# A decoder layer on one core: how far ahead the scores run, when weights are squared, and where small tiles lie

## The chip, the cores and the metric

The kernel runs on one core of a Trainium2 chip. A core has TensorE (PE) for matmuls, whose results land in PSUM, a memory of eight banks; VectorE (DVE), ScalarE (ACT) and GpSimd (POOL) for elementwise work; and DMA queues, here issued by SyncE (SP). The engines run side by side, each takes its own instructions strictly in order, and semaphores make one wait for another. The metric is the device time of one execution in microseconds, lower is better.

## The reference

One pre-norm decoder layer on x of 8 batches x 128 tokens x 512 features in fp32:

```python
x = x + _L0_attn_ref(_layernorm(x), w_q, w_k, w_v, w_o)
x = x + _L0_xattn_ref(ctx, ctx, _layernorm(x))
x = x + _L0_ffn_ref(_layernorm(x), gate_*, up_*, down_*)
```

The first line is causal self-attention with 32 query heads of 128 features in 8 groups; the four query heads of a group share one key and value head. The second is a small attention of x over ctx for each batch. The third is a gated FFN, 512 to 1376 and back, whose three weight matrices come as packed 4-bit words: of each int32, nibble k is shifted out and masked, a zero point plus one is taken off, and the rest is multiplied by a scale for each group of 128 rows.

## The kernel before

**Precision and the cost of it.** Matmuls are in fp16, with each operand split into a high and a low half; `mm3` (L160 to L166) does one product as three matmuls, high x high (L164), high x low (L165) and low x high (L166). `split` (L117) makes the halves: a cast on ACT (L118), a subtraction on DVE or POOL (L121). Weights come in fp32. Before they are split they are scaled by a power of two, which comes from their sum of squares: `sumsq` (L244) squares a block on ACT and adds it up along the row (L262), `scales_parts` (L276) casts the sums on DVE (`sb`, L285), adds them over the partitions with a one-column matmul into a PSUM tile `ps_n` (L289, L292) and makes the scale on DVE (L298, L306, L314). `soft_scale` (L327) makes from the scales of q and k the factor that goes into the softmax: two small multiplications (L331) and a reciprocal (L339) on DVE. `convert` (L350) then multiplies the weights on POOL (L355) and splits them, cast on ACT, subtraction on POOL: `wqh`/`wql`, `wkh`/`wkl`, `woh`/`wol`. The raw q weights of a group (`rawq`, 1 MB) and the raw output weights (`rawo`) have one buffer each, so the next group's fetch waits until the last conversion has read it.

**Steps.** The attention is 64 steps, one for each head group and batch (`steps`, L1051). A step has three parts on PE:
- `att_s` (L587): the scores, 12 small matmuls into `ps_sc`; masking and row maximum on DVE (L608), exponentials on ACT (L565), sums' reciprocal on DVE (L573), the multiplications on POOL (L575, L622), a split into `pb`, and a DMA that transposes `pb` to `pt` (L636).
- `att_v` (L639): `pt` times the values, five matmuls into `ps_at` (the first at L645), evicted to `ah` (ACT) and `al` (DVE).
- `att_o` (L653): `ah`, `al` times the output weights, 12 matmuls of 512 columns into `ps_o`, and the residual update `xr` on DVE (L662).
Beside these a step carries a piece of the projections of a later group (`proj_piece`, L1111: 12 matmuls of 512 columns for one query head, at times those of k or of v too).

**How far ahead.** `step` (L1367) issues `att_s` and `proj_piece` of step i + 1 up to step SOON = 14, of i + 2 from there to BACK = 42, and of i + 1 again afterwards; at step BACK itself none is issued. From step TAIL = 53 on `tail_step` (L1335) takes over, again with a distance of one, and adds the cross-attention and the start of the FFN. The loop at L1387 issues behind each step what was booked for it: with `at` (L1117) the fetches, squares, scales and conversions of later groups (L1120 to L1147), with `at_x` (L1062) the loads, squares and scales of ctx (`c_load`, `sumsq("c")`, `c_prep`, L1065 to L1068), and from step 8 to step 42 one `dequant` chunk each, 35 in all.

**Dequantization.** `dequant` (L785) loads a chunk of packed words (`qr`) and its zero points (`zi`) by DMA; DVE shifts and masks (L807) into the SBUF tile `qi` (one buffer) and subtracts (L811) into the fp16 weights `nfg`, `nfu`, `nfd`.

**PSUM.** `bank` (L189) hands out banks by tag: two each for "j" (projections), "s" (scores), "a" (`ps_at`, `ps_n` and later the transposes of the output) and "o" (`ps_o`).

**Who sets the order.** The Tile framework schedules: the code's order is a priority, and each engine's instructions are put where the framework expects them to be ready. `in_order` pins an order by hand, for all engines at the start and for PE and POOL from step 52 on; `issue_after` (L124) puts one instruction behind another of its engine, so the squares behind the exponentials of their step and the conversions behind the softmax's multiplications (`pace`). What the scheduler made of it is read from the built program.

Of the kernel before, what the change touches and what calls it, by code (L numbers as in the profile page):

```python
# [12 lines left out]
I32 = mybir.dt.int32  # L13
# [4 lines left out]
P = 128  # L18
HQ = 64
B = 8  # L20
H = 512
KT = 4
NG = 8
GH = 4
# [29 lines left out]
def tile_decoder(  # L54
# [129 lines left out]


    psum = pool("psum", space=PSUM)
    BANKS = {"j": 2, "s": 2, "a": 2, "o": 2}

    def bank(tag, shape, name):  # L189
        return psum.tile(shape, F32, name=name, tag=tag, bufs=BANKS[tag])  # L190


# [83 lines left out]
    def scales_parts(kind, g, cols=None):  # L276

        ss = raw_t["ss", kind, g]  # L280
        n = ss.shape[1]
        c0, c1 = cols or (0, n)
        m = c1 - c0
        sb = small.tile([P, m], BF16, name="sb", tag=f"sb{m}")
        nc.vector.tensor_copy(sb, ss[:, c0:c1])  # L285
        ps = bank("a", [P, GH], "ps_n")
        w = m if kind == "q" else 1
        if w == m:
            nc.tensor.matmul(ps[:, :w], ones, sb, start=True, stop=True)  # L289
        else:  # L290
            for i in range(m):
                nc.tensor.matmul(  # L292
                    ps[:, :1], ones, sb[:, i : i + 1], start=i == 0, stop=i == m - 1
                )
        yield
        norm = ONORM if kind == "o" else WNORM
        r = small.tile([P, w], F32, name="r", tag=f"r{w}")
        nc.vector.tensor_scalar(  # L298
            r.bitcast(I32),
            ps[:, :w].bitcast(I32),  # L300
            0x7F000000,
            1,
            ALU.bitwise_and,
            ALU.logical_shift_right,
        )
        nc.vector.tensor_scalar(r, r, ROOT, 2.0**64 / norm, ALU.max, ALU.mult)  # L306
        if kind == "c":
            sc_t[kind, g] = scx[:, g : g + 1]
        if (kind, g) not in sc_t:
            sc_t[kind, g] = small.tile(  # L310
                [P, GH if kind == "q" else 1], F32, name="sc" + kind, tag="sc" + kind
            )
        sc = sc_t[kind, g]
        nc.vector.reciprocal(sc[:, c0:c1] if kind == "q" else sc, r)  # L314
        yield
# [11 lines left out]
    def soft_scale(g):  # L327
        two = small.tile([P, GH // 2], F32, name="soft", tag="soft")
        for i in range(2):
            rows = slice(i * HQ, (i + 1) * HQ)  # L330
            nc.vector.tensor_scalar(  # L331
                two[rows],
                sc_t["q", g][rows].rearrange("p (a i) -> p a i", i=2)[:, :, i],
                sc_t["k", g][rows],
                -(ASCALE**2) / SCALE,
                ALU.mult,
                ALU.mult,
            )
        nc.vector.reciprocal(two, two)  # L339
        soft_t[g] = two  # L340
# [444 lines left out]
    def dequant(m, g, c0, c1, after, pts=None):  # L785
        qsrc = quant[m][0]
        n = c1 - c0
        rows = min(16, qsrc.shape[0] - g * 16)
        p = rows * 8
        qr = deqp.tile([P, H], I32, name="qr", tag="qr", bufs=2)  # L790
        load_q = nc.sync.dma_start(
            qr[:p, :n],
            qsrc[g * 16 : g * 16 + rows, c0:c1]
            .rearrange("r n -> r () n")
            .to_broadcast([rows, 8, n]),
        )
        zi = deqp.tile([P, H], I32, name="zi", tag="zi", bufs=2)
        row = zrow[m] + g
        load_z = nc.sync.dma_start(
            zi[:p, :n],  # L800
            zt["d"][row : row + 1, c0:c1].to_broadcast([p, n]),
        )
        if pts:
            issue_after(load_q, pts)
            issue_after(load_z, pts)
        qi = deqp.tile([P, H], I32, name="qi", tag="qi", bufs=1)
        ins = nc.vector.tensor_scalar(  # L807
            qi[:p, :n], qr[:p, :n], sh[:p], 15, ALU.logical_shift_right, ALU.bitwise_and
        )
        issue_after(ins, after)  # L810
        nc.vector.scalar_tensor_tensor(  # L811
            nf[m][:p, g, c0:c1], qi[:p, :n], -1.0, zi[:p, :n], ALU.add, ALU.subtract
        )
# [250 lines left out]

    for b in range(B):  # L1065
        at_x(XC + b, lambda b=b: c_load(b))
        at_x(XC + b + 1, lambda b=b: sumsq("c", b, 0, 0))
        at_x(XC + b + 3, lambda b=b: c_prep(b))  # L1068
        done = steps.index((NG - 1, b))
        tail_x.setdefault((done + 1, 0), []).append(lambda b=b: xA(b))  # L1070


        if b >= HB:
            if b % 2:
                two = b - 1, b
                tail_x.setdefault((done + 2, 1), []).append(
                    lambda two=two: [xB(b) for b in two]
                )
                tail_x.setdefault((done + 3, 2), []).append(
                    lambda two=two: [(xC(b), h3_load(b)) for b in two]  # L1080
                )
            continue
        tail_x.setdefault((done + 2, 1), []).append(lambda b=b: xB(b))
        tail_x.setdefault((done + 3, 2 if b < HB - 1 else 0), []).append(
            lambda b=b: (xC(b), h3_load(b))
        )
# [33 lines left out]
    for g in range(1, NG):  # L1120
        u0 = units.index((g, 0))
        c = HB * (u0 - 2) - (g > 2)
        if g > 1:
            m = c - HB
            at(m, lambda g=g: fetch_wk(g))
            at(m + 1, lambda g=g: (fetch_wq(g), sumsq("k", g, 0, 0)))
            at(m + 2, lambda g=g: (sumsq("q", g, 0, 0), sumsq("q", g, 0, 1)))
            at(m + 3, lambda g=g: (sumsq("q", g, 0, 2), sumsq("q", g, 0, 3)))
            at(m + 3, lambda g=g: (scales("q", g), scales("k", g), soft_scale(g)))
        for j in range(GH):  # L1130
            at(c + j, lambda g=g, j=j: prep_wq(g, j))
        at(c + 1, lambda g=g: prep_wk(g))
        c = HB * (u0 - 1)
        m = c - HB
        at(m, lambda g=g: fetch_wo(g))
        at(m + 1, lambda g=g: sumsq("o", g, 0, 0, 2))
        at(m + 2, lambda g=g: sumsq("o", g, 1, 0, 2))
        at(m + 3, lambda g=g: (scales("o", g), out_scale(g)))
        for j in range(GH):
            at(c + j, lambda g=g, j=j: prep_wo(g, j))  # L1140
        if g % 2 == 0:
            c = HB * (u0 - 3) - (g > 2)
            at(c - 2, lambda g=g: fetch_wv(g // 2))
            at(c - 1, lambda g=g: sumsq("v", g // 2, 0, 0))
            at(c, lambda g=g: scales("v", g // 2))
            at(c + 2, lambda g=g: prep_wv(g // 2, 0))
            at(c + 3, lambda g=g: prep_wv(g // 2, 1))  # L1147
# [214 lines left out]
        for f in tail_x.pop((i, 1), ()):  # L1362
            f()

    SOON, BACK = 14, 42

    def step(i):  # L1367
        g, b = steps[i]
# [17 lines left out]
    soft_scale(1)  # L1386
    for i in range(len(steps)):  # L1387
        known = len(nc.cur_bb.bb.instructions)
        if i == XC:
            deqp.release()  # L1390
            xc = pool("xc", 2, side="right", reuse_waits="tile")
        if i == FFN_MEM:
            rawp.release()
            fp = pool("fp", 2, reuse_waits="tile")
            xa = pool("xa", 2, reuse_waits="tile")
        if i == FFN0:
            xt.update(s="a", o="a")
        pace["dma"] = pt_dma[steps[i + 1]] if i >= TAIL and steps[i + 1 :] and steps[i + 1] in pt_dma else None
        paced = (tail_step if i >= TAIL else step)(i)
        pace["exp"], pace["mul"] = paces[steps[i + (SOON < i < min(BACK, len(steps) - 1))]]  # L1400
        for f in todo.pop(i, ()):
            f()
        if 3 <= i < 6:
            col_scales("gud"[i - 3], paced)
        if i == 0:
            zeros_load()
        if i == 1:
            scales_load()
        if 1 <= i < 5:
            zeros((2 * (i - 1), 2 * (i - 1) + 1), paced)  # L1410
        if i == 5:
            zeros_store()
        if i in chunk_steps:
            dequant(*chunks[chunk_steps.index(i)], paced, pt_dma[steps[i + 1]] if i == chunk_steps[0] else None)
        if i == 6:
            inter_scale()
        for f in x_steps.pop(i, ()):
            f()
        if i < 5 * HB:
            traced_after(known, last_h.ins.engine, last_h)  # L1420
        if i == TAIL - 1:
            pins = [in_order((e,)) for e in (mybir.EngineType.PE, mybir.EngineType.Pool, )]
            for pin in pins:
                pin.__enter__()
        if i == FFN0 - 1 + 0:
            pins[0].__exit__(None, None, None)
# [60 lines left out]
```

## Time and profile before

| what | value |
|---|---|
| three runs | 656.52, 656.67, 656.84 us; median 656.67 |
| the profiled execution | 655.96 us, its span 654.2 us |
| granted PE clock | 0.998 of full speed |
| first PE matmul of step 0's, 20's, 42's and 53's `att_v` | 53.7, 203.9, 361.0, 452.0 us |
| DVE: unpacking, L807, 128x512 | 26 x 725 ns |
| DVE: subtraction, L811, 128x512 | 26 x 792 to 955 ns |
| DVE: soft factor, L331 | 16 x 412 ns |
| ACT: square of 128x512, L262 | 627 ns and 188 ns for reading the sum |
| DMA: rawq, 1 MB | 5.8 us from issue to landing |
| DMA: pt | 2.7 us from issue to landing |

The span runs from the first to the last instruction of the profiled execution. "Busy" is the time in which an engine has an instruction under way; for PE, whose matmuls overlap, a row's duration is longer than its distance to the next one, so the start times tell more than the durations. In a group's line, the idle time is that of its engine just before the group's instructions, with what ended it. A line of the code can be that of a helper, so tiles are named beside it.

### The profile page before, as it was taken

What the parts mean: (1) busy time and instruction counts of PE and PEld (TensorE: products, weight loads), DVE (VectorE), ACT (ScalarE), POOL (GpSimd) and SP (SyncE); (2) the same over time, 40 slices, a digit from 0 to 9 for tenths busy, and PEclk for the clock granted to TensorE, in tenths of its full rate; (3) what the DMA queues carried; (4) which work ended last, traced back from release to release, by engine and by line L of the source; (5) the groups of instructions that cost most, each with busy time, mean ns of one, the idle gap of its engine ahead of it and who ended that gap; (6) DMA issues with size and microseconds to landing.
All of it is one profiled execution on the core that took longest, in us unless ns stands there. A gap on an engine that the chain in (4) does not pass through costs nothing.

```text
span 654.2 us, 12431 instructions
## 1 busy us (share of the span) xinstructions
PE 629.8 (96%) x3992; PEld 342.3 (52%) x3992; DVE 465.6 (71%) x1475; ACT 439.3 (67%) x1238; POOL 380.8 (58%) x586
## 2 busy tenths in 40 slices
PE   8789999999999999999999999999999989999996
PEld 6455545565655555565555465556544434445443
DVE  6846676665767866576777555767776768988986
ACT  5687677465667675566667576866566478867674
POOL 7757477563747883475489395734577247612521
PEclk9999999999999999999999999999999999999999
DMA  9287254943763756355636414343544242102002
GB/s 316 48 171 170 75 72 122 229 105 79 190 164 88 187 137 160 95 168 127 151 94 167 143 41 122 66 92 74 89 67 68 39 93 50 31 19 65 1 1 64
DMA packets 117773, 69.34 MB, mean 106 GB/s; under 512 B 84190, under 2 KB 100593, under 8 KB 117708
## 3 DMA queue, kind: packets, MB, share of 16 engines
q1 hardware_dynamic: 117708, 68.55, 44.0%
q8 instruction: 31, 0.51, 0.3%
q14 instruction: 34, 0.28, 0.2%
HBM read 42.12 MB, written 2.20 MB: 68 GB/s over the span
## 4 chain that ended last, share of the span: by engine, by line
PE 73%; DVE 8%; DMA 6%; ACT 6%; POOL 4%; issue 2%; SPq 1%; DVEq 0%; ACTq 0%; POOLq 0%
PE ps_o L166 7%; PE ps_o L164 7%; PE ps_o L165 7%; PE ps_q L164 7%; PE ps_q L165 7%; PE ps_q L166 7%; PE ps_c L1181 6%; PE ps_c L1182 6%; DMA rawq<-in_L_attn_w_q_dram 3%; DMA pt<-pb 2%; PE ps_v L164 2%; PE ps_v L166 2%; PE ps_v L165 2%; PE ps_k L165 2%; PE ps_k L166 2%
## 5 line engine op out<-in xcount | busy, mean ns | idle before, releaser
L565 ACT ACTIVATE s<-s,negm 128x64 f32<-128x64 f32 (+1 forms) x256 | 93.1, 365 | 51.5 <-DVE negm L608 50.8
L164 PE MATMUL ps_q<-hT,wqh 128*128 128x512 f16 (+1 forms) x260 | 97.7, 376 | 1.6 <-DVE ql L121 1.6
L164 PE MATMUL ps_o<-woh,ah 128*128 128x512 f16 x256 | 97.0, 379 | 1.2 <-ACT ah L118 1.2
L166 PE MATMUL ps_o<-woh,al 128*128 128x512 f16 x256 | 96.9, 379 | 1.1 <-DVE al L121 1.1
L166 PE MATMUL ps_q<-hT,wql 128*128 128x512 f16 (+1 forms) x260 | 97.7, 376 | 0.0
L165 PE MATMUL ps_q<-hT,wqh 128*128 128x512 f16 (+1 forms) x260 | 97.7, 376 | 0.0
L165 PE MATMUL ps_o<-wol,ah 128*128 128x512 f16 x256 | 97.0, 379 | 0.0
L121 POOL TENSOR_TENSOR pb<-s,pb 128x256 f16<-128x256 f32 (+1 forms) x128 | 72.6, 582 | 16.2 <-ACT pb L118 14.3
L662 DVE SCALAR_TENSOR_TENSOR xr<-ps_o,unsc,xr 128x512 f32<-128x512 f32 x64 | 47.8, 747 | 41.3 <-PE ps_o L166 34.4
L575 POOL TENSOR_SCALAR rec<-rec 128x4 f32<-128x4 f32 x64 | 14.2, 222 | 108.1 <-DVE rec L573 87.5
L121 DVE TENSOR_TENSOR ql<-ps_q,qh 128x512 f16<-128x512 f32 x64 | 44.0, 688 | 40.3 <-ACT qh L118 40.2
L608 DVE CUSTOM_DVE_ANT_0 s<-ps_sc,mask,soft 128x64 f32<-128x64 f32 (+1 forms) x256 | 67.1, 310 | 4.0 <-PE ps_sc L166 1.9
L622 POOL TENSOR_TENSOR s<-s,rec 128x128 f32<-128x128 f32 (+1 forms) x128 | 63.6, 518 | 4.8
L118 ACT CAST pb<-s 128x256 f16<-128x256 f32 (+1 forms) x128 | 42.8, 349 | 28.1 <-POOL s L622 24.7
L118 ACT CAST ah<-ps_at 128x512 f16<-128x512 f32 x64 | 37.2, 582 | 21.9 <-PE ps_at L166 15.9
L565 ACT ACTIVATION_READ_ACCUMULATOR s<-s,negm 128x1 f32 x256 | 48.0, 188 | 0.0
L121 DVE TENSOR_TENSOR al<-ps_at,ah 128x512 f16<-128x512 f32 x64 | 43.7, 683 | 3.4 <-ACT ah L118 2.9
L1194 DVE TENSOR_SCALAR ps_c<-ps_c,rTg 128x512 f32<-128x512 f32 (+1 forms) x56 | 40.7, 750 | 7.0 <-PE ps_c L1182 6.4
L1192 ACT ACTIVATE ps_c<-ps_c,rTu 128x512 f32<-128x512 f32 (+1 forms) x57 | 36.2, 659 | 11.4 <-PE ps_c L1182 9.3
L118 ACT CAST qh<-ps_q 128x512 f16<-128x512 f32 x64 | 36.6, 571 | 10.6 <-PE ps_q L166 9.6
L166 PE MATMUL ps_sc<-k,ql 128*128 128x128 f16 (+1 forms) x256 | 42.6, 206 | 0.5 <-DVE ql L121 0.5
L165 PE MATMUL ps_sc<-k,qh 128*128 128x128 f16 (+1 forms) x256 | 41.5, 206 | 0.0
(244 smaller groups left out, 1698.3 us busy)
## 6 DMA issues: line engine op xcount, KB each, us to landing
rawq<-in_L_attn_w_q_dram SPq DMA_DIRECT2D x8, 1024.0 KB, 5.8
rawo<-in_L_attn_w_o_dram SPq DMA_DIRECT2D x8, 1024.0 KB, 6.1
zi<-zd SPq DMA_DIRECT2D x26, 256.0 KB, 4.1
vd<-v SPq DMA_DIRECT2D x64, 64.0 KB, 2.4
qr<-_L_ffn_down_qweight_dram SPq DMA_DIRECT2D x10, 256.0 KB, 5.8
xr<-in_x_dram SPq DMA_DIRECT2D x8, 256.0 KB, 8.2
rawk<-in_L_attn_w_k_dram SPq DMA_DIRECT2D x8, 256.0 KB, 5.7
rawv<-in_L_attn_w_v_dram SPq DMA_DIRECT2D x4, 512.0 KB
```

Of the source, the lines that this page charges most:

```text
L118: a = nc.scalar.copy(hi, src)
L121: b = (lo_eng or nc.vector).tensor_tensor(lo, src, hi, ALU.subtract)
L164: nc.tensor.matmul(ps, lh, rh, start=start and i == 0, stop=False)
L165: nc.tensor.matmul(ps, lh, rl, start=False, stop=False)
L166: nc.tensor.matmul(ps, ll, rh, start=False, stop=stop and i == n - 1)
L565: exp = nc.scalar.activation(v, v, AF.Exp, bias=negm[:, j : j + 1], scale=-1.0, accum_out=sums[:, j : j + 1],)
L608: nc.vector.tensor_tensor_reduce(view, flat(ps, cols[j]), masks[j // 2], soft_t[g][:, j % 2 : j % 2 + 1], BIG, ALU.add, ALU.min, negm,)
L622: mul = nc.gpsimd.tensor_tensor(v, v, rec[:, 2 * k : 2 * k + 2].unsqueeze(2).to_broadcast([P, 2, (k + 1) * HQ]), ALU.mult,)
L662: return nc.vector.scalar_tensor_tensor(xr[b], ps, unsc_t[g], xr[b], ALU.mult, ALU.add)
L1181: nc.tensor.matmul(ps, lh, rh, start=r == 0, stop=False, skip_group_check=r > 0)
L1182: nc.tensor.matmul(ps, lh, rl, start=False, stop=True, skip_group_check=r > 0)
L1194: nc.vector.tensor_scalar(ps, ps, sc, None, ALU.mult)
```

## The change

Five things are edited:
- BACK goes from 42 to 52: the scores and projections of steps 44 to 53 are issued one step earlier than before.
- Bookings move. The q fetch of group 2 goes one step later, that of group 7 two steps. The q squares of group 7 go to step 44, two of them from 41 and two from 42; its scales and soft factor go from 42 to 44; its q conversions go one step later. The k squares of groups 2 to 7, the o squares of all groups and the ctx squares go one step later.
- `qi` is no longer an SBUF tile: the unpacked words lie in a PSUM bank with the new tag "d".
- Tag "a" has one bank and "d" the other. Before step 8 and from step 43 on, `bank` hands out "a" and "d" in turn for what asks for "a"; between, `ps_at` has "a" alone, and `ps_n` of `scales_parts` shares "d" with the words.
- The two multiplications of `soft_scale` are on GpSimd for groups 2 to 7.

No matmul is added or removed.

```diff
-    BANKS = {"j": 2, "s": 2, "a": 2, "o": 2}
+    BANKS = {"j": 2, "s": 2, "a": 1, "d": 1, "o": 2}
+    flip = [0, True]
     def bank(tag, shape, name):
+        if tag == "a" and flip[1]:
+            flip[0] += 1
+            tag = "ad"[flip[0] % 2]
         return psum.tile(shape, F32, name=name, tag=tag, bufs=BANKS[tag])
...
-        ps = bank("a", [P, GH], "ps_n")
+        ps = bank("a" if flip[1] else "d", [P, GH], "ps_n")
...
-            nc.vector.tensor_scalar(
+            (nc.gpsimd if g > 1 else nc.vector).tensor_scalar(
                 two[rows],
...
-        qi = deqp.tile([P, H], I32, name="qi", tag="qi", bufs=1)
+        qi = bank("d", [P, H], "ps_d").bitcast(I32)
...
-        at_x(XC + b + 1, lambda b=b: sumsq("c", b, 0, 0))
+        at_x(XC + b + 2, lambda b=b: sumsq("c", b, 0, 0))
...
             at(m, lambda g=g: fetch_wk(g))
-            at(m + 1, lambda g=g: (fetch_wq(g), sumsq("k", g, 0, 0)))
-            at(m + 2, lambda g=g: (sumsq("q", g, 0, 0), sumsq("q", g, 0, 1)))
-            at(m + 3, lambda g=g: (sumsq("q", g, 0, 2), sumsq("q", g, 0, 3)))
-            at(m + 3, lambda g=g: (scales("q", g), scales("k", g), soft_scale(g)))
+            n = m + 5 if g == NG - 1 else m + 3
+            at(n - 2 if g > 2 else n - 1, lambda g=g: fetch_wq(g))
+            at(m + 2, lambda g=g: sumsq("k", g, 0, 0))
+            at(n - (g < NG - 1), lambda g=g: (sumsq("q", g, 0, 0), sumsq("q", g, 0, 1)))
+            at(n, lambda g=g: (sumsq("q", g, 0, 2), sumsq("q", g, 0, 3)))
+            at(n, lambda g=g: (scales("q", g), scales("k", g), soft_scale(g)))
         for j in range(GH):
-            at(c + j, lambda g=g, j=j: prep_wq(g, j))
+            at(c + j + (g == NG - 1), lambda g=g, j=j: prep_wq(g, j))
...
-        at(m + 1, lambda g=g: sumsq("o", g, 0, 0, 2))
-        at(m + 2, lambda g=g: sumsq("o", g, 1, 0, 2))
+        at(m + 2, lambda g=g: sumsq("o", g, 0, 0, 2))
+        at(m + 3, lambda g=g: sumsq("o", g, 1, 0, 2))
...
-    SOON, BACK = 14, 42
+    SOON, BACK = 14, 52
...
+        if i == chunk_steps[0]:
+            flip[1] = False
         if i == XC:
+            flip[1] = True
             deqp.release()
```

In the booking code g is the group, c the step of its first conversion and m = c - 4; for group 7 m is step 39.

## The prediction

> **What bounds the kernel now.** I read the page first, then the busy times by stage, then TensorE (PE) around its longest pauses, then the chain behind them.
>
> ```profile
> PE 629.8 (96%) x3992; PEld 342.3 (52%) x3992; DVE 465.6 (71%) x1475; ACT 439.3 (67%) x1238; POOL 380.8 (58%) x586
> ```
>
> PE is busy nearly always, and its matmuls are pipelined, so only where it pauses can an edit that leaves its matmuls alone gain anything. The busy times by stage say where that is (columns: window, its length, then busy us of PE, PEld, DVE, ACT, POOL, the granted clock, DMA share, GB/s):
>
> ```profile
> 60.00:360.00 300.00, 299.21 (x1984) 165.93 (x1983) 207.76 (x710) 196.71 (x637) 193.86 (x305) 1.00 0.55 135
> 360.00:380.00 20.00, 17.69 (x122) 9.75 (x121) 11.22 (x46) 12.63 (x41) 9.31 (x16) 1.00 0.43 126
> 380.00:455.00 75.00, 75.00 (x509) 42.79 (x507) 48.48 (x207) 51.71 (x163) 46.05 (x73) 1.00 0.35 80
> 455.00:560.00 105.00, 97.99 (x609) 49.30 (x608) 78.74 (x248) 70.84 (x181) 58.96 (x91) 1.00 0.39 68
> ```
>
> From 60 to 455 us PE idles 3.1 us, 2.3 of them between 360 and 380. The timeline of PE there shows four waits (start, duration; the last bracket is the idle time and what ended it):
>
> ```profile
> 368.02 0.19 PE L166 MATMUL ps_sc<-k,ql 128*128 128x64 f16 x1
> 368.79 0.39 PE L164 MATMUL ps_o<-woh,ah 128*128 128x512 f16 x1 [0.57 <-ACT ah L118]
> 369.01 0.38 PE L165 MATMUL ps_o<-wol,ah 128*128 128x512 f16 x1
> ...
> 370.11 0.39 PE L166 MATMUL ps_o<-woh,al 128*128 128x512 f16 x1 [0.47 <-DVE al L121]
> ...
> 377.99 0.28 PE L645 MATMUL ps_at<-pt,vd 128*128 128x256 f16 x1 [0.63 <-DMA pt<-pb]
> ...
> 379.63 0.39 PE L164 MATMUL ps_o<-woh,ah 128*128 128x512 f16 x1 [0.64 <-ACT ah L118]
> ```
>
> A 512-column matmul lasts 0.38 us but the next starts 0.22 us after it (368.79, 369.01), a 64-column one 0.03 us after it. So the loss is the start-to-start distance less that: 0.74, 0.62, 0.79 and 0.80 us, **2.95 us**. By the first matmul of each step (L645, one per step) this is steps 42 to 45. The chain through the place reads:
>
> ```profile
> 356.60 2.75 POOL wql L121 x2
> 359.74 5.84 DMA rawq<-in_L_attn_w_q_dram
> 365.60 0.73 ACT junk L262 x2
> ```
>
> GpSimd finishes the last two weight splits of group 6, which frees the only rawq buffer; then group 7's fetch starts; and ScalarE, whose next instruction is the square of those weights, stands still:
>
> ```profile
> 365.60 0.63 ACT L262 ACTIVATE junk<-rawq 128x512 bf16<-128x512 f32 x1 [4.57 <-DMA rawq<-in_L_attn_w_q_dram]
> ```
>
> Behind it in ScalarE's queue are the eviction ah of step 42 and the exponentials of step 44; their lateness is what PE meets.
>
> **The change part by part.**
>
> *Squares and fetch of group 7 later.* For g = 7 the fetch goes from step 40 to 42, the eight instructions (activate and accumulator read) of the q squares from steps 41 and 42 to 44, scales and soft factor from 42 to 44, the four conversions one step on. In the built program's order ScalarE now has, between the last weight cast of group 6 and the first square, a k cast, twice four exponentials, one square of rawo, an ah, two pb casts and a qh: by the spacings of their rows (0.47, 1.45 twice, 1.05, 0.48, 0.75, 0.47) 6.1 us of work, and step 45's scores have to pass PE first. Against it stand the split (1.13), the issue (0.4) and the transfer (5.84): 7.4 us. The 4.57 us wait falls to 0 to 1.3 us, and the late ah and exponentials go. On SP the fetch now stands behind step 43's transpose instead of ahead of it; that transpose's data come from GpSimd before the split, so it isn't held up. For g = 3 to 6 the fetch stays; k and o squares go one step on; for g = 2 the fetch goes one step on: all in stretches where PE has no idle time, 0.
>
> *Distance of two up to step 52.* Scores (12 small matmuls, 0.5 us) and the projection of steps 44 to 53 come one step earlier. In steps 15 to 41, which have this distance, PE never waited on pt; at 42 to 46 the transposed probabilities landed less than 1.5 us ahead of their use. So the 0.79 us wait on pt goes too. What is late next: the projections of group 7 are due a step earlier while their weights come a step or two later, and GpSimd is full there (from 377.40 to 394.4 without a gap). In the new order PE has about 24 us of matmuls from the end of step 46's scores to the first k matmul that needs wkl (blocks of twelve at 2.6, v at 1.3, at at 0.55, scores at 0.5); GpSimd has 4 us of softmax ahead of it and 17.3 us of work (conversions 0.74, splits 1.13, s pairs 0.95, pb pairs 1.02, rec 0.2). Slack 2.7 us: I take 0 and keep +2. From step 53 to step 62 the order on PE, GpSimd, ScalarE and DVE is that of before, so the 7.0 us idle in 455 to 560 stay; only the ctx scores of batch 4 come 2 us earlier. 0, bounds -1.5 and +1.5 (by the four waits of 0.3 to 1.1 us at 535 to 546).
>
> *Unpacked words in PSUM.* L807 now writes PSUM, L811 reads it. Neither form is in the trace. L807 (mean 725 ns, 26 of 512) is bounded by its own median, 546, and by L1194, which reads and writes PSUM (751). L811 (792 to 955) is bounded by its minimum, 679, and L662 (PSUM and SBUF in, 750). I take 700 and 730, the PSUM ends being nearest: about 35 x 0.15 = 5 us less of DVE, bounds -10 and +1. DVE is busy 207.76 of 300 us in this stretch, beside PE: worth 0. Without that cover each pair would count with its 1.5 us.
> The trace has 512 words at 546 ns and 352 at 392, which is 1.07 to 1.11 ns each, and no shorter row. The Trainium skill (VectorE: DVE Perf Modes, Why PSUM operands drop a tier) speaks against this edit: any PSUM operand takes away the mode that reads one tensor through both SBUF ports. Were the unpack in such a mode now it would double, some 19 us of DVE; the rows show no such mode to lose, and either way DVE would stay below PE.
>
> *One bank for ps_at, one shared by words and ps_n* (steps 8 to 42). A ps_at must wait for the previous step's al: 0.48 + 0.60 us after its last matmul, while in the new order at least two blocks of twelve (5.2 us) lie between. 0. A ps_n must wait for the last L811; see the rivals.
>
> *Soft factors on GpSimd*: 12 instructions of 412 ns leave DVE (4.9 us); on GpSimd they cost what rec L575 does, 222 ns (2.7 us). Bounds: 143 (L575 on DVE) to 1119 ns (slowest L331). The reciprocal behind them on DVE waits for GpSimd's queue, with a residual update and the next scores behind it; in the new order 0 (group 2) to 9 DVE instructions stand between the last scale and it. PE is several matmul blocks away from these: 0, up to +0.5.
>
> *Step 5's wait on pt* (0.79 us at 88.5): at5 stands five q matmuls earlier, and the residual update that the zeros' store and that pt wait for comes earlier by as much. 0, bounds -0.9 and +0.2.
>
> **Sum.** -2.95, +0.25 for what remains of ScalarE's wait: -2.7 us. The profiled execution took 655.96 us (span 654.2 and 1.8 around it), 0.7 below the median of the runs, 656.67. So 655.96 - 2.7 = 653.3, and on the scale of the runs **654.0 us**.
>
> **Rivals.** A difference of 0.2%, 1.3 us, is about what a measurement of this kernel can tell from no change.
> *A. The stall moves* (20%): wkl or the last wql of group 7 comes late, as GpSimd has slack of 2.7 us and DVE can hold it up; or the batch-4 scores meet a qT that hasn't landed. 2 us of the gain go back: 656.0 (655.4 to 658.0). For: GpSimd's 17 full us. Against: before, these conversions lay equally thick and PE idled 0.00 there.
> *B. Slower* (14%): PE at ps_n. With the words in bank d, 14 of the small ps_n matmuls between steps 8 and 42 wait for DVE to finish an L811, and PE, in order, waits with them. It decides where DVE reaches that L811 later than PE reaches ps_n. A wait is up to a pair, 1.6 us, 0.8 on average; seven of them 5.6, less 2.7: 659.5 (658 to 663). Against: DVE waited for ps_n (xr 3.7 us on L289), PE for its input sb only 1.3 us, before 50 us.
> *C. More* (10%): the batch-4 scores shorten the FFN start and step 5's wait goes: 651.5.
> That the change does nothing (the fetch can't start before the split, whichever step issues it) is part of A.
>
> **Numbers.** Forecast 652.5 to 655.3: 56%; A 20%, B 14%, C 10%. Range: the forecast, A and the upper half of C, 652.0 to 658.0. Faster by over 0.2%: forecast and C, 0.66; within: 0.20; slower: 0.14.
>
> **What would show it.** PE idle in 360 to 380 under 0.7 us; ScalarE's wait for rawq under 1.5; L807 and L811 with little spread near 0.7; no wait of PE on ps_n; 75 us from step 46 on still without idle. PE waits on wkl, ps_n or pt between 100 and 455 us would make it wrong.

## The result and the profile after

The changed kernel takes **660.25 us** in the median of nine runs (658.44 to 663.14), the kernel before 656.52 (655.97 to 657.47, nine runs beside them). The ratio is 1.0054, 95% interval 1.0038 to 1.007: slower by about 3.6 us, where 2.7 us of gain were forecast. The changed kernel's profiled execution took 660.25 us, its span is 658.5 us, against 654.2 before.

The page of the changed kernel says of the engines, first:

```profile
PE 632.1 (96%) x3992; PEld 343.5 (52%) x3992; DVE 455.1 (69%) x1463; ACT 438.8 (67%) x1238; POOL 377.3 (57%) x598
```

PE has the same 3992 matmuls, DVE is busy 10.5 us less, and none of this says why it is slower. The busy times by stage do (columns as before: window, length, busy us of PE, PEld, DVE, ACT, POOL, granted clock, DMA share, GB/s):

```profile
60.00:360.00 300.00, 298.77 (x1992) 165.75 (x1991) 197.14 (x699) 197.45 (x640) 191.22 (x317) 1.00 0.54 133
360.00:380.00 20.00, 20.00 (x131) 11.41 (x129) 12.97 (x46) 12.60 (x46) 4.55 (x10) 1.00 0.59 147
380.00:455.00 75.00, 72.03 (x469) 39.92 (x468) 44.70 (x192) 48.82 (x149) 47.06 (x74) 0.98 0.31 72
455.00:560.00 105.00, 96.31 (x614) 48.94 (x612) 78.11 (x252) 69.18 (x183) 58.93 (x92) 1.00 0.40 68
```

In 360 to 380 PE is busy without a gap, where it idled 2.3 us before: the forecast gain is there. In 380 to 455, where it had no gap, it now idles 3 us and issues only 469 matmuls instead of 509, at a clock of 0.98. The timeline of PE shows the places (the first lines after the pause, then two lines from step 52):

```profile
437.54 0.39 PE L164 MATMUL ps_o<-woh,ah 128*128 128x512 f16 x1 [1.69 <-ACT ah L118]
...
439.25 0.63 PE L166 MATMUL ps_o<-woh,al 128*128 128x512 f16 x1
439.68 0.63 PE L164 MATMUL ps_o<-woh,ah 128*128 128x512 f16 x1
...
448.28 0.27 PE L166 MATMUL ps_at<-pt,v 128*128 128x256 f16 x1
449.23 0.39 PE L164 MATMUL ps_o<-woh,ah 128*128 128x512 f16 x1 [0.68 <-ACT ah L118]
```

PE waits 1.69 us for `ah`; then its 512-column matmuls stand 0.43 us apart (439.25, 439.68) instead of 0.22 for 3.4 us, at half the clock. From 438.49 to 442.12 nine of them take 3.63 us instead of 9 x 0.216 = 1.94, so the slow clock costs 1.7 us more. At 449 `ps_o` stands directly behind the `ps_at` of its own step, with no projection between them that would cover the eviction. ScalarE's timeline says why `ah` was late, and SyncE's when the transfer that ScalarE waited for was issued:

```profile
436.29 0.63 ACT L266 ACTIVATE junk<-c 128x512 bf16<-128x512 f32 x1 [1.64 <-DMA c<-in_ctx_dram]
436.83 0.19 ACT L266 ACTIVATION_READ_ACCUMULATOR junk<-c 128x1 f32 x1
436.92 0.57 ACT L118 CAST ah<-ps_at 128x512 f16<-128x512 f32 x1
```

```profile
433.45 0.51 SPq L978 DMA_DIRECT2D c<-in_ctx_dram  x1
```

The last ctx block was fetched at 433.45; its square, in ScalarE's queue ahead of `ah`, waited for it. It is the same figure as at 365 before: a square that waits for its weights, with an eviction behind it. Only the tile is another.

For all runs below I sum, as in the prediction, start-to-start distances of PE beyond those of a matmul of that width: **PE's loss**, by stretch. The time lost to a slow clock is in it.

| run | what it is | median us | ratio to before (95%) | 360-380 | 380-460 | 460-end |
|---|---|---|---|---|---|---|
| before | | 656.5 | 1 | 3.1 | 0.1 | 15.0 |
| after | everything | 660.25 | 1.0054 (1.0038-1.0070) | 0.0 | 5.6 | 16.4 |
| e1 | after, ctx squares as before | 659.5 | 1.0041 (1.0029-1.0054) | 0.0 | 4.2 | 16.7 |
| e2 | after, BACK = 42 | 660.7 | 1.0064 (1.0039-1.0089) | 0.0 | 4.9 | 16.7 |
| e3 | before, all bookings and BACK = 52 | 662.0 | 1.0077 (1.0061-1.0092) | 0.0 | 8.5 | 15.1 |
| e4 | before, group 7 moved | **653.8** | 0.9954 (0.9941-0.9968) | 0.0 | 1.0 | 15.0 |
| e5 | after, o squares as before | 660.9 | 1.0062 (1.0049-1.0075) | 0.0 | 5.7 | 16.5 |
| e6 | e4 and later o squares | 655.5 | 0.9984 (0.9975-0.9992) | 0.0 | 0.9 | 15.1 |
| e7 | e4 and BACK = 52 | 660.7 | 1.0060 (1.0048-1.0072) | 0.0 | 8.4 | 15.0 |
| e8 | before, words and banks in PSUM | 659.1 | 1.0042 (1.0026-1.0058) | 0.0 | 3.8 | 16.4 |
| e9 | e7, five ctx buffers | 655.6 | 0.9980 (0.9969-0.9991) | 0.0 | 2.3 | 15.0 |
| e10 | after, five ctx buffers | 660.2 | 1.0054 (1.0038-1.0070) | 0.0 | 4.5 | 16.6 |
| e11 | e4, five ctx buffers | 654.6 | 0.9966 (0.9954-0.9978) | 0.0 | 1.1 | 15.0 |
| e12 | e4 and BACK = 48 | 660.4 | 1.0059 (1.0044-1.0073) | 0.0 | 6.9 | 15.0 |
| e13 | before, banks alone | 662.9 | 1.0089 (1.0073-1.0104) | 4.0 | 1.9 | 16.5 |
| e14 | e4 and soft factors on GpSimd | 658.05 | 1.0030 (1.0013-1.0047) | 1.0 | 1.9 | 15.2 |
| e15 | e3, five ctx buffers | 657.0 | 0.9998 (0.9989-1.0008) | 0.0 | 2.4 | 15.0 |
| e16 | before, BACK = 52 alone | 656.5 | 1.0000 (0.9984-1.0015) | 1.8 | 1.8 | 15.0 |
| e17 | e7, conversions behind step i | 656.2 | 0.9994 (0.9981-1.0007) | 0.0 | 1.6 | 15.7 |
| e18 | after, conversions behind step i | 661.6 | 1.0076 (1.0059-1.0093) | 0.0 | 8.9 | 16.5 |

Each run stood beside runs of the kernel before of its own, with medians from 656.47 to 657.02 us, so rows are best compared by their ratios. The losses are each from one profiled execution; those of e2, e8 and e18 are from the slowest of their runs (663.97, 661.56 and 664.12 us). In the line of after against before they add up: -3.1 + 5.5 + 1.4, and +0.4 at step 5, make 4.2 us, and the spans differ by 4.3.

### The profile page after: what moved, and what is told of

Its sections match the earlier page's. It is cut to its first block, busy times and chain, and to the rows that moved or that the text cites. A ratio compares the mean times of both kernels' runs of the same rounds, so it can differ in the third digit from the quotient of the medians.

```text
span 658.5 us, 12414 instructions
## 1 busy us (share of the span) xinstructions
PE 632.1 (96%) x3992; PEld 343.5 (52%) x3992; DVE 455.1 (69%) x1463; ACT 438.8 (67%) x1238; POOL 377.3 (57%) x598
## 4 chain that ended last, share of the span: by engine, by line
PE 72%; POOL 7%; ACT 6%; DMA 6%; DVE 5%; issue 3%; SPq 0%; DVEq 0%; POOLq 0%; ACTq 0%
PE ps_o L166 7%; PE ps_o L165 7%; PE ps_o L164 7%; PE ps_c L1187 7%; PE ps_c L1188 7%; PE ps_q L164 7%; PE ps_q L166 7%; PE ps_q L165 7%; DMA qT<-hb 2%; DMA pt<-pb 2%; PE ps_k L164 2%; PE ps_k L166 2%; PE ps_k L165 2%; PE ps_v L164 2%; PE ps_v L165 2%
## 5 line engine op out<-in xcount | busy, mean ns | idle before, releaser
L121 POOL TENSOR_TENSOR pb<-s,pb 128x256 f16<-128x256 f32 (+1 forms) x128 | 69.2, 554 | 17.7 <-ACT pb L118 15.6
L118 ACT CAST qh<-ps_q 128x512 f16<-128x512 f32 x64 | 37.0, 578 | 16.4 <-PE ps_q L166 15.4
L166 PE MATMUL ps_sc<-k,ql 128*128 128x64 f16 (+1 forms) x256 | 43.5, 207 | 0.9 <-DVE ql L121 0.5
L165 PE MATMUL ps_sc<-k,qh 128*128 128x64 f16 (+1 forms) x256 | 41.6, 207 | 0.0
```

The lines of the kernel that those rows point to most:

```text
L118: a = nc.scalar.copy(hi, src)
L121: b = (lo_eng or nc.vector).tensor_tensor(lo, src, hi, ALU.subtract)
L165: nc.tensor.matmul(ps, lh, rl, start=False, stop=False)
L166: nc.tensor.matmul(ps, ll, rh, start=False, stop=stop and i == n - 1)
```

## The experiments

### First: which edit brings the new stall (e1 to e4)

Theory 1 was what the lines above suggest: the ctx squares, booked one step later, put ScalarE behind a late ctx transfer. Theory 2 blamed the distance of two, theory 3 the banks. e4 was the priced step of the prediction by itself.

e1, from the changed kernel:

```diff
-        at_x(XC + b + 2, lambda b=b: sumsq("c", b, 0, 0))
+        at_x(XC + b + 1, lambda b=b: sumsq("c", b, 0, 0))
```

e2, from the changed kernel:

```diff
-    SOON, BACK = 14, 52
+    SOON, BACK = 14, 42
```

e3 is the kernel before with BACK = 52 and all the booking lines of the change. e4, from the kernel before, has those of group 7 alone:

```diff
+            n = m + 5 if g == NG - 1 else m + 3
-            at(m + 1, lambda g=g: (fetch_wq(g), sumsq("k", g, 0, 0)))
-            at(m + 2, lambda g=g: (sumsq("q", g, 0, 0), sumsq("q", g, 0, 1)))
+            at(n - 2, lambda g=g: fetch_wq(g))
+            at(m + 1, lambda g=g: sumsq("k", g, 0, 0))
+            at(n - (g < NG - 1), lambda g=g: (sumsq("q", g, 0, 0), sumsq("q", g, 0, 1)))
...
-            at(c + j, lambda g=g, j=j: prep_wq(g, j))
+            at(c + j + (g == NG - 1), lambda g=g, j=j: prep_wq(g, j))
```

> The changed kernel, but with the ctx squares one step after their load, as before. Theory 1 (the later ctx squares put ScalarE behind a late ctx transfer, so the eviction ah of step 50 comes 1.7 us late and PE stops at 437): the stall of 5.6 us in 420 to 455 goes, about 655 us, 0.998 of the kernel before. Theory 2 (the distance of two up to step 52 does it) and theory 3 (the PSUM banks and the soft factors shift the scheduler's order there): the stall stays, 659 to 661 us.

> The changed kernel, but with BACK = 42, so the scores of steps 44 to 53 run one step ahead as before. Theory 2 (distance): the stall in 420 to 455 goes, and PE waits on pt near 378 may come back (0.8 us), about 655 us. Theories 1 (later ctx squares) and 3 (banks, soft factors): the stall stays, 659 to 661 us.

> The kernel before with BACK = 52 and all the moved bookings, but with the words in SBUF, two banks for tag a and the soft factors on VectorE, as before. Theory 3 (banks or soft factors shift the order around steps 49 to 52): the stall in 420 to 455 goes while the gain at 360 to 380 stays, about 654 us. Theories 1 and 2 (ctx squares, distance): 659 to 661 us.

> The kernel before with the fetch, squares, scales and conversions of group 7 alone moved. The prediction's priced step by itself: the four waits of PE at 368 to 380 (2.95 us) go, except the one on pt (0.8 us), which the distance of one may keep: 653.7 to 654.5 us, 0.996 to 0.997 of before. If the stall only moves: 656 us or more.

Measured: 659.5, 660.7, 662.0 and 653.8 us. Theories 1, 2 and 3 all fall in the form in which I held them: in none of e1, e2 and e3 does the stall go. e4 lands on its expectation. Its stages, and ScalarE at the first square of rawq, which comes without a wait:

```profile
360.00:380.00 20.00, 20.00 (x136) 11.44 (x135) 12.50 (x43) 12.75 (x41) 10.54 (x18) 1.00 0.50 130
380.00:455.00 75.00, 74.43 (x507) 42.12 (x505) 50.09 (x215) 52.99 (x165) 45.12 (x73) 1.00 0.35 80
```

```profile
366.96 0.62 ACT L262 ACTIVATE junk<-rawq 128x512 bf16<-128x512 f32 x1
```

So one part of the change holds the whole forecast gain, and something else in it loses more than twice as much.

### Second: single parts added to the good one (e5 to e8)

In the changed kernel GpSimd waits 9.16 us at 371 for `sco`, the scale of group 6's output weights. Theory 4: the later o squares do this, and GpSimd's backlog delays all that follows. Theory 5: no single booking, but the distance of two together with the later group 7.

e5, from the changed kernel (e6 makes the reverse edit in e4):

```diff
-        at(m + 2, lambda g=g: sumsq("o", g, 0, 0, 2))
-        at(m + 3, lambda g=g: sumsq("o", g, 1, 0, 2))
+        at(m + 1, lambda g=g: sumsq("o", g, 0, 0, 2))
+        at(m + 2, lambda g=g: sumsq("o", g, 1, 0, 2))
```

e7 is e4 with `BACK = 52`. e8 is the kernel before with the lines of the change on `BANKS`, `flip`, `bank`, `ps_n` and `qi`.

> The changed kernel, but with the o squares one and two steps after their fetch, as before. Theory 4 (the later o squares make GpSimd wait 9 us at 371 for the scale sco of group 6; its backlog then delays the fetch of rawo for group 7 from 399 to 404 and, through ScalarE, PE at 437): GpSimd's wait falls to about 3 us, rawo of group 7 is fetched before 400, the stall in 420 to 455 goes, 655 to 656 us. Theory 5 (no single booking: the distance of two together with a later group 7 leaves GpSimd's work too late whichever squares move): the stall stays, 659 to 661 us.

> The kernel before with the move of group 7 (653.8 us by itself) and the o squares one step later, nothing else. Theory 4 (o squares): GpSimd waits longer for sco of group 6 and a stall of 4 to 6 us comes in 400 to 455, 657 to 660 us. Theory 5 (needs the distance of two too): 653.5 to 655 us.

> The kernel before with the move of group 7 and BACK = 52, with every other booking, the banks and the soft factors as before. Theory 4 (o squares): no stall, 653 to 654.5 us. Theory 5 (distance and group 7 together): a stall of 4 us or more in 400 to 455, 657 to 661 us.

> The kernel before with the words in a PSUM bank and the banks of tags a and d, nothing else. If the banks cost nothing, as predicted: 656 to 657 us, the four waits at 368 to 380 as before. If the banks are what adds 0.45 us at step 5 and about 1.5 us behind 460 in the changed kernel, as its trace beside the run without banks (where these are as before) says: 658 to 659 us.

Measured: 660.9, 655.5, 660.7 and 659.1 us. Theory 4 falls: with the old o squares the stall stays (e5), and the new ones bring none in 400 to 455 (e6; its 1.7 us over e4 are mostly a new wait on pt of 1.1 us at 124). Theory 5 holds: the two edits that I had priced at -2.7 and 0 make +4.2 us together (e7). And the banks with the words in them, priced at 0, cost 2.7 us (e8). In e8 the old stall at 360 to 380 is gone without any booking moved, and a new one of 3.8 us stands in 400 to 440.

### Third: how the distance of two does it (e9 to e12, e17)

e7 is the small kernel in which to see it. ScalarE's waits there, in all and three times in the timeline, and SyncE's ctx fetches beside them:

```profile
ACT junk L262 <- DMA c<-in_ctx_dram: 5.4, 3, 2.3
```

```profile
438.45 0.63 ACT L262 ACTIVATE junk<-c 128x512 bf16<-128x512 f32 x1 [1.96 <-DMA c<-in_ctx_dram]
...
443.11 0.63 ACT L262 ACTIVATE junk<-c 128x512 bf16<-128x512 f32 x1 [2.31 <-DMA c<-in_ctx_dram]
...
444.97 0.35 ACT L565 ACTIVATE s<-s,negm 128x64 f32<-128x64 f32 x1 [1.14 <-DVE negm L608]
...
448.89 0.58 ACT L118 CAST ah<-ps_at 128x512 f16<-128x512 f32 x1
```

```profile
435.56 0.52 SPq L974 DMA_DIRECT2D c<-in_ctx_dram  x1
...
440.60 0.33 SPq L974 DMA_DIRECT2D c<-in_ctx_dram  x1
```

Each fetch is issued 2.9 and 2.5 us ahead of the square that needs it, no sooner, because a ctx block's buffer comes free only when the block three batches earlier has been converted. That conversion needs a scale, the scale a square, the square its fetch. Eight batches go round this loop of three buffers, and the exponentials and `ah` stand behind its squares on ScalarE. Theory 6: this loop holds PE. Theory 7: the step without scores, which moves from 42 to 52, is what the engines miss.

The same line is changed in e7 (e9), in the changed kernel (e10) and in e4 (e11); e12 is e4 with `BACK = 48`:

```diff
-        raw_t["c", b] = c = xc.tile([P, H], F32, name="c", tag="c", bufs=3)
+        raw_t["c", b] = c = xc.tile([P, H], F32, name="c", tag="c", bufs=5)
```

> The kernel before with the move of group 7, BACK = 52, and five buffers instead of three for the loaded ctx blocks. Theory 6 (three ctx buffers make a loop: the load of batch b + 3 waits for the conversion of batch b, its square waits for the load, and ah and the exponentials stand behind that square on ScalarE; the distance of two starts this loop late and PE reaches it): ScalarE waits under 1.5 us for c, the PE waits at 435, 441 and 449 go, 653.5 to 655.5 us. Theory 7 (the step without scores, which moves from 42 to 52, is what is missed, since GpSimd, VectorE and ScalarE have no softmax to do there): 658 to 661 us, as with three buffers.

> The changed kernel with five buffers instead of three for the loaded ctx blocks. Theory 6 (loop of three ctx buffers): the stall of 5.6 us in 420 to 455 goes, what the banks cost stays, 655 to 657 us. Theory 7 (the missing free step): 659 to 661 us.

> The kernel before with the move of group 7 and five ctx buffers, BACK = 42. Both theories: 653.0 to 654.2 us, as with three buffers (653.8), since PE loses only about 1 us in 400 to 455 there; if the ctx loop is what holds that 1 us, 653.0.

> The kernel before with the move of group 7 and BACK = 48, three ctx buffers. Theory 7 (the step without scores lets the other engines catch up): with it at 48, in the middle of the crowded stretch, 654 to 657 us. Theory 6 (the loop of three ctx buffers starts late because of the distance of two in steps 42 to 47): 658 to 661 us.

Measured: 655.6, 660.2, 654.6 and 660.4 us. Two more buffers take 5.1 us from e7 (e9, 0.1 us above the range that theory 6 gave), and ScalarE waits for no ctx block there: theory 6 is shown for e7, and theory 7 falls, with e12 as well. They gain nothing in e4 (e11): ScalarE waits 5.1 us for c with three buffers and 2.6 with five, but PE loses only about 1 us in 380 to 460 either way. They do not help the whole changed kernel either (e10): the wait at 437 goes, but others come in its place, and the last section of experiments is about those. What is left in e9 is one crowd on ScalarE (its timeline, then PE's):

```profile
411.15 1.06 ACT L262 ACTIVATE junk<-rawo 128x1024 bf16<-128x1024 f32 x1 [2.35 <-DMA rawo<-in_L_attn_w_o_dram]
...
414.05 1.05 ACT L262 ACTIVATE junk<-rawo 128x1024 bf16<-128x1024 f32 x1
```

```profile
420.25 0.20 PE L164 MATMUL ps_sc<-k,qh 128*128 128x64 f16 x1 [1.03 <-ACT qh L118]
```

The raw output weights of group 7 come late, ScalarE waits 2.35 us for them, and two of their squares and five ctx squares then stand ahead of the `qh` that PE wants. So in e7 and e9 everything from rawo on starts late. GpSimd's last split of group 6's output weights, which frees rawo, says from when on; e4 first, then e7:

```profile
396.10 1.16 POOL L121 TENSOR_TENSOR wol<-rawo,woh 128x512 f16<-128x512 f32 x1
```

```profile
403.48 1.15 POOL L121 TENSOR_TENSOR wol<-rawo,woh 128x512 f16<-128x512 f32 x1
```

It is 7.4 us later, about one step, though PE had not lost more by then: in e7 the first `att_v` of all comes at 53.2 us and the loss from 60 to 400 is 1.05 us, in e4 53.8 and 1.07. BACK stands in one more line of the loop over the steps, which the diff does not show because its text is unchanged: it picks the step behind whose softmax squares, conversions and ctx casts are put. Theory 8: with BACK = 52 they go behind the softmax of step i + 1 in steps 42 to 51, and this anchor makes them late, not the scores.

e17 edits that line in e7, e18 in the changed kernel:

```diff
-        pace["exp"], pace["mul"] = paces[steps[i + (SOON < i < min(BACK, len(steps) - 1))]]
+        pace["exp"], pace["mul"] = paces[steps[i + (SOON < i < min(42, len(steps) - 1))]]
```

> The kernel before with the move of group 7 and BACK = 52 (660.7 us), but the conversions, squares and ctx casts of steps 42 to 51 put behind the softmax of step i, as with BACK = 42. Theory 8 (the anchor: BACK also puts them behind the softmax of step i + 1, one step later, so the fetch of rawo and the ctx loop start a step late): rawo is fetched before 400, the stall in 400 to 455 falls under 2 us, 654 to 656 us. Theory 9 (the scores that run ahead fill the engines in any order): the stall stays, 659 to 661 us.

> The changed kernel with the conversions, squares and ctx casts of steps 42 to 51 put behind the softmax of step i, as with BACK = 42. Theory 8 (the anchor): the stall of 5.6 us in 420 to 455 shrinks to 2 us or less, what the banks cost elsewhere (about 2 us) stays, 655.5 to 657.5 us. Theory 9, or banks and order that hold it by themselves: 659 to 661 us.

e17 took 656.2 us, 4.5 less than e7, and PE's loss in 380 to 460 falls from 8.4 to 1.6: theory 8 is right about the stall, if not in every number (the time is 0.2 us above its range). The last split of group 6 stands at 399.81, halfway between e4 and e7, and rawo is fetched at 401.2, not before 400. e18 took 661.6 us: in the whole changed kernel the anchor does not help.

### Fourth: the banks, the soft factors, the distance alone (e13 to e16)

e13 has the banks but leaves the words in SBUF. e14 adds the soft factors to e4. e15 is e3 with five ctx buffers, that is the changed kernel's bookings and distance without banks and soft factors. e16 has BACK = 52 and nothing else. The edits are lines shown above.

> The kernel before with the banks of tags a and d handed out as in the changed kernel, but the unpacked words in SBUF as before. If the banks cost (PE's order around them shifts, 0.45 us at step 5 and 1.5 us behind 460): 658 to 660 us, as with the words (659.1). If the words cost: 656 to 657 us.

> The kernel before with the move of group 7 and the two multiplications of the soft factors on GpSimd. As predicted, soft factors cost 0 to 0.5: 653.5 to 654.5 us (653.8 without them). If they hold up the scales behind them: 656 us or more.

> The kernel before with all the moved bookings, BACK = 52 and five ctx buffers, but without the banks, the words in PSUM and the soft factors. If the banks hold the whole changed kernel with five ctx buffers (660.2): 655 to 656.5 us, as with the move of group 7 and BACK = 52 alone (655.6). If the other bookings (squares of k, o and ctx one step later) hold it: 658.5 to 661 us.

> The kernel before with BACK = 52 alone. Theory 6 (the distance of two starts the ctx work late and the loop of three buffers holds PE): the four waits at 368 to 380 go or shrink and a stall of 4 us or more stands in 400 to 455, 658 to 662 us. If the distance costs only together with the later group 7: 653.5 to 657 us.

Measured: 662.9, 658.05, 657.0 and 656.5 us.

e13: the banks alone cost 0.9%, more than banks and words together (659.1). In the eight kernels that have the banks, PE loses 16.4 to 16.7 us behind 460, and in all the others 15.0 to 15.7. The waits of PE on two of the tiles there (455 to 575 us), in the kernel before and then in e13:

```profile
PE ps_xs L164 <- DMA qT<-hb: 0.5, 1, 0.5
PE ps_c L1181 <- ACT ps_c L1192: 0.6, 1, 0.6
```

```profile
PE ps_xs L164 <- DMA qT<-hb: 2.6, 3, 1.4
PE ps_c L1185 <- ACT ps_c L1196: 2.4, 3, 1.3
```

Nothing waits for `ps_n` or an unpacked word there. The built program shows that the scheduler puts PE's matmuls in another order once the banks are handed out otherwise, from step 0 on (53.6 us). At the FFN's start the twelve matmuls of the scores of batch 4 then stand ahead of step 63's `att_v` and of eight FFN matmuls, instead of behind them; PE reaches three such blocks of scores before their qT has landed. This order is the same in e8, e13 and the changed kernel, and the old one is the same in before and e4. Why the scheduler orders them so is not settled.

e14: the soft factors cost 4.2 us over e4. From 60 to 456 us PE's waits are on pt, none on the factors; in e4 those on pt are one of 0.8 us. Why pt comes later is not shown.

```profile
PE ps_at L645 <- DMA pt<-pb: 4.4, 4, 1.5
```

e15 against e10: without banks and soft factors the changed kernel with five ctx buffers takes 657.0 instead of 660.2 us. So the banks and soft factors hold those 3.2 us. The two traces show most of it: 1.6 us of loss behind 460, the order at the FFN's start, and 2.2 us at two steps where e10 has `ps_o` directly behind `ps_at`, as at 449 in the changed kernel, while e15 has 0.3 us there, with three matmuls of a projection between the two at 446.8. One of the two places in e10:

```profile
443.10 0.27 PE L166 MATMUL ps_at<-pt,v 128*128 128x256 f16 x1
444.05 0.39 PE L164 MATMUL ps_o<-woh,ah 128*128 128x512 f16 x1 [0.68 <-ACT ah L118]
```

e15 against e3 is the test of theory 6 once more: two more buffers take 662.0 to 657.0 us.

e16: the distance alone costs and gains nothing measurable, and theory 6's forecast for it, 658 to 662 us, fails. It takes a part of the old stall (3.1 to 1.8 us) and brings 1.8 us in 380 to 460. The last split of group 6 stands at 400.42 there, about where e17 has it, so the late anchor needs the later group 7 to bring the stall.

## Why the prediction was wrong, step by step

**Squares and fetch of group 7: right.** Forecast -2.95 and +0.25 for what remains; e4 measures 0.46% less, about 3.0 us, and in the changed kernel PE's loss in 360 to 380 falls from 3.1 to 0.0. ScalarE's wait for rawq went from 4.57 to 0. One reading was off: by the count of L645 the four waits lie in steps 42 and 44, none in 45.

**"What is late next: the projections of group 7 ... Slack 2.7 us: I take 0 and keep +2": the step that failed.** PE never waits on `wkl` or `wql` in the changed kernel. Late was what comes behind those conversions on GpSimd: the last splits of group 6's output weights, through them the fetch of rawo, and behind it the ctx loop on ScalarE. The two edits make +4.2 us where I had -2.7 (e7); with the loop opened -1.4 (e9 against its before), with the anchor left alone -0.3 (e17). Two things could have been read in advance. The wait view of ScalarE before (380 to 456 us) shows three waits for c of 3.6 us together, and I passed over them since PE had no gap there:

```profile
ACT junk L262 <- DMA c<-in_ctx_dram: 3.6, 3, 2.2
```

And BACK is used in the `pace` line too.

**"k and o squares ... all in stretches where PE has no idle time, 0": wrong in kind.** No gap on PE says that the others were in time, not by how much. Added to e4, the o squares cost 1.7 us (e6); taken back from the changed kernel they gain nothing (e5, 660.9). The ctx squares, which I had not priced, make 0.8 us in the medians (e1), within the intervals.

**"One bank for ps_at, one shared by words and ps_n ... 0": wrong.** 5.9 us for the banks alone (e13), 2.7 with the words (e8). Rival B had a cost here, and the measured 660.25 us lies in its range, but by luck: PE does not wait at `ps_n` anywhere behind 60 us in the changed kernel. In e1, e2, e5, e8 and e18 it does, up to 2.0 us at 414 (e2), but behind step 42, when no word lies in the bank, and not for an L811. The order moves instead. The earlier scores of batch 4, which I had seen and put at 0 with bounds of -1.5 and +1.5, are this order: with all that shifts behind 460 they are the 1.4 us of the table.

**Words in PSUM: right in size, wrong in the reading behind it.** Forecast 700 and 730 ns and about 5 us less DVE. By form, the wide tile (for the subtraction that of `nfd`), before and then after:

```profile
L807 DVE TENSOR_SCALAR qi<-qr,sh 128x512 int32<-128x512 int32 x26 | 18.9, 725 | 0.5 <-DMA qr<-_L_ffn_gate_qweight_dram 0.5
L811 DVE SCALAR_TENSOR_TENSOR nfd<-qi,zi 128x512 f16<-128x512 int32 x10 | 9.5, 955 | 0.1
```

```profile
L811 DVE TENSOR_SCALAR ps_d<-qr,sh 128x512 int32<-128x512 int32 x26 | 19.4, 745 | 0.5 <-DMA qr<-_L_ffn_gate_qweight_dram 0.5
L815 DVE SCALAR_TENSOR_TENSOR nfd<-ps_d,zi 128x512 f16<-128x512 int32 x10 | 6.8, 682 | 0.0
```

The unpacking takes 745 ns in the mean (725 before), the subtraction 680 to 685 (792 to 955). Over the 26 wide pairs that is 0.5 us more and 4.9 less. But the means hide two effects, and "512 words at 546 ns ... and no shorter row" was a misreading: 546 ns is the median over all widths. The rows by length (ns, least, median, greatest, all widths), before and then after:

```profile
L807 DVE TENSOR_SCALAR qi<-qr,sh x35: 392/546/1422, 114.2 to 364.3; 128x512 int32<-128x512 int32 x26, 128x352 int32<-128x352 int32 x8, 96x512 int32<-96x512 int32 x1
```

```profile
L811 DVE TENSOR_SCALAR ps_d<-qr,sh x35: 571/744/753, 111.7 to 370.6; 128x512 int32<-128x512 int32 x26, 128x352 int32<-128x352 int32 x8, 96x512 int32<-96x512 int32 x1
```

Before, the eight wide rows during which GpSimd has no instruction under way take 474 to 478 ns; the other 18 take 477 to 1422, 836 in the mean. After, all 26 take 743 to 753, whatever GpSimd does. From 352 to 512 words the shortest rows grow by 82 ns before (392 to 474) and by 172 after (571 to 743). So there was a faster mode to lose, and it is lost: this agrees with the Trainium skill (VectorE: DVE Perf Modes, Why PSUM operands drop a tier), which says that an operand in PSUM takes it away. What is won in its place is that GpSimd's instructions no longer stretch these rows; the subtraction went from 672 to 693 ns alone and up to 1640 beside GpSimd to 674 to 692 in all rows. That this is worth nothing in time is not shown by itself: no run has the words in PSUM without the new banks, and e8, which has both, takes 3.8 us less than e13, with another order of PE as well.

**Soft factors: their length right, their worth wrong.** 261 ns each on GpSimd against a forecast 222; but +4.2 us over e4 in e14, where I had 0 to +0.5.

**Rivals and range.** Rival A, the stall that moves, named the right kind of thing, but at 2 us and with the wrong transfer; it measures 5.5 us. The range ended at 658.0 because rival A was priced as one late wait and rival B was left out of it. None of five single edits of the changed kernel (e1, e2, e5, e10, e18) brings it below 659 us: several of its parts bring a stall into 380 to 455, each without the others (e7, e8), and their costs do not add up. e7 and e8 would make 660.7 + 2.7 = 663; the whole makes 660.25. Two things together hold the 3.6 us: with the ctx loop opened and without banks and soft factors (e15) the kernel takes 657.0 us, as before the change, while the first alone leaves 660.2 (e10) and the second alone 662.0 (e3). Why the scheduler chooses the orders that cost, and what else keeps e15 3.2 us above e4 beside the o squares, stays open.

The best version found is e4: the move of group 7 without the rest, 653.8 us, 0.9954 of before (0.9941 to 0.9968).

## What to carry to other kernels

Where a scheduler makes the order, an edit that is worth nothing by its own durations can cost more than the one it rides on: run the priced part by itself first, and treat every "0" that changes the order as a cost of unknown sign. A bottleneck engine without gaps does not mean that the engines behind it have slack. Look at their own waits on transfers, and count how many buffers the loop behind such a wait has. When a constant changes, follow every use of it, the unchanged lines too.

## What the runs showed of the hardware

The clock of PE halves after pauses shorter than I had expected, and not every time. All these kernels have the same pause of 2.5 us of PE at about 29. In the kernel before, the clock stays full behind it; in the changed one it falls to half for 3.4 us (the stretch 29 to 32 of before, then of after; the clock is the third number from the right):

```profile
29.00:32.00 3.00, 3.00 (x40) 2.75 (x41) 2.46 (x11) 2.09 (x6) 2.80 (x3) 1.00 0.48 90
```

```profile
29.00:32.00 3.00, 3.00 (x28) 2.50 (x26) 1.35 (x4) 1.61 (x3) 2.39 (x3) 0.50 0.49 90
```

Half the clock follows that pause in 12 of the 20 profiled executions. It also follows the pause of 1.69 us at 437 in the changed kernel, 2.0 us in e12, 2.7 in e7 and 3.0 in e3, but not those of 1.8 and 1.6 us in e13, nor of 2.0 us in e2 (at 414) and in e18 (at 412).

The clock records say more than the length of a pause. Every stretch at full clock that ends in a half one is a multiple of 3.413 us long (23.89 us is 7 of them; 406.19, in the changed kernel, 119; 443.73, in e7, 130). So the clock falls only on a grid of 3.413 us, which begins with the first rise, 4.4 to 7.3 us into the execution. In each window of the grid up to 600 us I count the share that PE's matmuls fill, each with its usual distance to the next. All 17 falls follow a window filled by 0.13 to 0.40, and of the windows up to 0.40 only one other, of 0.38 in e10, has no fall behind it. The pause at 29 lies within one window in the changed kernel (0.21, from 25.6) and is cut in two in the kernel before (0.72 from 23.8, 0.49 from 27.2). The Trainium skill (TensorE: Matmul & The Clock Gate, Part 1: The HAM clock gate) says that the activity window of 3413 ns runs freely, which agrees with this; its rule that it takes an idle window of about 3.4 us does not, since windows filled by up to 0.40 were enough.

At 437 the slow clock costs 1.7 us. At 29 it costs nothing in the end: the 130th matmul behind the pause starts 14.6 us after it at full clock and 16.0 to 16.3 us after it where the clock fell, but the first `att_v` comes 24.4 to 26.3 and 24.5 to 25.1 us after it, since PE waits for others in between. So this pause does not explain why the changed kernel scatters more between runs (658.4 to 663.1 us against 656.0 to 657.5); nor do the mean clocks of its runs, 0.996 and 0.997 in the two slowest, 0.991 in one of 660.25 us. That stays open.
